# Reordering the opening of a four-layer graph network by hand: chunk 0's transfer first, degrees ahead of the norms, W1's tile on bytes of its own, masks later

## Chip, cores, metric

One core of a Trainium2 chip. The metric is the device time of one execution in microseconds (us). Every profile named here covers one execution, with times counted from the start of its span. PE is the matmul engine (PEld its weight loads), DVE the vector, ACT the scalar, POOL the GpSimd and SP the sync engine, which here only issues transfers.

## The reference, cut to what matters

Four layers, each `x = x + layer(relu(layernorm(x)))`, on x of 128 x 64 x 256 (fp32), with one 64 x 64 adjacency. Only layer 0's beginning and layer 1's beginning matter here:

```python
h = jnp.maximum(_layernorm(x, axis=-1), 0.0)
# layer 0
A_norm = A + jnp.eye(n)
deg = jnp.sum(A_norm, axis=0) + jnp.sum(A_norm, axis=1) - jnp.diagonal(A_norm)
dinv = jax.lax.rsqrt(deg)
A_hat = A_norm * dinv[:, None] * dinv[None, :]
agg = jnp.einsum('nm,bmd->bnd', A_hat, features)
h = jax.nn.relu(_batchnorm(agg @ W1.T + b1, g1, be1))   # 256 -> 512, then W2 back to 256
# layer 1: two graph convolutions with adj, then four LSTMs over windows of 1 to 4 steps
# layers 2 and 3: attention with masks made from the causal triangle and from adj
```

The 8,192 rows are worked in 16 chunks of 512 (512 KB each). Before the first product with W1 can start, chunks 0 and 1 must be normalised and aggregated with A_hat.

## The kernel before

A tile framework places the semaphores and orders instructions by its own estimate of time; inside a `manual_schedule` block the named engines keep the program's order among the block's instructions. Before, that held for PE alone.

```python
    for e in range(2):                                   # adjacency: block diagonal, and a second copy
        r = slice(e * T, (e + 1) * T)
        nc.sync.dma_start(adj_bd[r, r], adj)
        nc.scalar.dma_start(adjt_bd[r, r], adj_t)
        nc.sync.dma_start(adj2[r, :], adj)
    with tc.tile_pool(name="setup", bufs=1) as setup:    # freed before W1's tile is made
        ...                                              # an, ant, dg, deg: eight DVE operations
        rsqrt(dinv, deg[:, 3:4], 0.0)                    # two operations on POOL
        nc.vector.tensor_scalar(rows, an, dinv, None, op0=OP.mult)
        nc.tensor.transpose(pt[:, :P], rows, ident)
        nc.vector.tensor_scalar(ahat_t, pt[:, :P], dinv, None, op0=OP.mult)
        ...                                              # mask2, mask3
    # ... bn1, bn2 loads
    def aggregate(src, mat, name):
        for k in range(KD):
            for j in range(NJ):
                for i in range(2):
                    for e in range(2):
                        nc.tensor.matmul(banks[e][half(i), k, j, :], src[half(e), j, f],
                                         mat[half(e), half(e)], start=True, stop=True)
    # ...
        w1_sb = w0.tile([P, KD, H0], F32, name="w1_sb")  # takes over the setup's bytes
        nc.gpsimd.dma_start(w1_sb, w1t.rearrange("(k p) f -> p k f", p=P))
        nc.gpsimd.dma_start(w2_sb, w2t.rearrange("(k p) f -> p k f", p=P))
        with tc.manual_schedule(engines={mybir.EngineType.PE}):
            norm0(0)                                     # load x, stats on DVE, power on POOL, h on ACT
            norm0(1)
            aggregate0(0)
            for c in range(NCH):
                if c + 1 < NCH:
                    aggregate0(c + 1)
                if c + 2 < NCH:
                    norm0(c + 2)
                product1(c)
    # ... layer 1: its small weights on SP, seven LSTM weights of 1 MB each from POOL, x again on SP
```

Of the kernel before, what the change touches and what calls it, by code (L numbers as in the profile page):

```python
# [8 lines left out]
F32 = mybir.dt.float32  # L9
AF = mybir.ActivationFunctionType  # L10
OP = mybir.AluOpType
AX = mybir.AxisListType

P = 128
EPS = 1e-5
NEG = -1e30
# [3 lines left out]
def kernel(  # L20
# [22 lines left out]
    nc = tc.nc  # L43
    B, T, D = x.shape
    H0 = w1t.shape[1]
    KD = D // P
    KH = H0 // P
# [6 lines left out]
    NJ = CH // P  # L54
# [9 lines left out]
    const = ctx.enter_context(tc.tile_pool(name="const", bufs=1))  # L64
# [4 lines left out]
    def bank(name):  # L69
        return psum.tile([P, CH], F32, tag="ps", name=name)  # L70
# [7 lines left out]
    def rsqrt(dst, src, eps):  # L78

        nc.gpsimd.tensor_scalar(dst, src, eps, None, op0=OP.add)  # L80
        nc.gpsimd.tensor_tensor(dst, dst, mhalf[:, : dst.shape[1]], OP.pow)



    adj_bd = const.tile([P, P], F32, name="adj_bd")
    adjt_bd = const.tile([P, P], F32, name="adjt_bd")
    adj2 = const.tile([P, T], F32, name="adj2")
    nc.vector.memset(adj_bd, 0.0)
    nc.vector.memset(adjt_bd, 0.0)
    for e in range(2):  # L90
        r = slice(e * T, (e + 1) * T)
        nc.sync.dma_start(adj_bd[r, r], adj)
        nc.scalar.dma_start(adjt_bd[r, r], adj_t)
        nc.sync.dma_start(adj2[r, :], adj)


    ahat_t = const.tile([P, P], F32, name="ahat_t")

    mask2 = const.tile([P, T], F32, name="mask2")
    mask3 = const.tile([P, 2 * T], F32, name="mask3")  # L100
    with tc.tile_pool(name="setup", bufs=1) as setup:
        an = setup.tile([P, P], F32, name="an")
        ant = setup.tile([P, P], F32, name="ant")
        nc.vector.tensor_add(an, adj_bd, ident)
        nc.vector.tensor_add(ant, adjt_bd, ident)
        deg = setup.tile([P, 4], F32, name="deg")
        dg = setup.tile([P, P], F32, name="dg")
        nc.vector.tensor_mul(dg, an, ident)
        nc.vector.tensor_reduce(deg[:, 0:1], ant, AX.X, OP.add)
        nc.vector.tensor_reduce(deg[:, 1:2], an, AX.X, OP.add)  # L110
        nc.vector.tensor_reduce(deg[:, 2:3], dg, AX.X, OP.add)
        nc.vector.tensor_add(deg[:, 3:4], deg[:, 0:1], deg[:, 1:2])
        nc.vector.tensor_sub(deg[:, 3:4], deg[:, 3:4], deg[:, 2:3])
        dinv = setup.tile([P, 1], F32, name="dinv")
        rsqrt(dinv, deg[:, 3:4], 0.0)
        rows = setup.tile([P, P], F32, name="rows")
        nc.vector.tensor_scalar(rows, an, dinv, None, op0=OP.mult)
        pt = bank("pt_ahat")
        nc.tensor.transpose(pt[:, :P], rows, ident)
        nc.vector.tensor_scalar(ahat_t, pt[:, :P], dinv, None, op0=OP.mult)  # L120

        causal = setup.tile([P, P], F32, name="causal")
        nc.gpsimd.affine_select(
            out=causal, in_=adj_bd, pattern=[[-1, P]], compare_op=OP.is_ge, fill=NEG, base=0,
            channel_multiplier=1,
        )
        for e in range(2):
            r = slice(e * T, (e + 1) * T)
            nc.vector.tensor_copy(mask2[r, :], causal[r, r])
        for i in range(2):  # L130
            nc.vector.tensor_scalar(mask3[:, i * T : (i + 1) * T], adj2, 0.0, NEG, op0=OP.is_equal,
                                    op1=OP.mult)

    bn1_sb = const.tile([P, 3, KH], F32, name="bn1_sb")
    bn2_sb = const.tile([P, 3, KD], F32, name="bn2_sb")
    nc.gpsimd.dma_start(bn1_sb, bn1)
    nc.gpsimd.dma_start(bn2_sb, bn2)


    def layernorm_relu(dst, src, name):  # L140
        st = small.tile([P, NJ, 6], F32, tag="ln_st", name=f"st_{name}")
        mv = small.tile([P, NJ, 2], F32, tag="ln_mv", name=f"mv_{name}")
        for j in range(NJ):
            nc.vector.bn_stats(st[:, j, :], src[:, j, :])
            nc.vector.bn_aggr(mv[:, j, :], st[:, j, :])
        rstd = small.tile([P, NJ], F32, tag="ln_rstd", name=f"rstd_{name}")
        rsqrt(rstd, mv[:, :, 1], EPS)
        nmr = small.tile([P, NJ], F32, tag="ln_nmr", name=f"nmr_{name}")
        nc.vector.scalar_tensor_tensor(nmr, mv[:, :, 0], -1.0, rstd, op0=OP.mult, op1=OP.mult)
        for j in range(NJ):  # L150
            nc.scalar.activation(dst[:, j, :], src[:, j, :], AF.Relu, bias=nmr[:, j : j + 1],
                                 scale=rstd[:, j : j + 1])

    def half(r):
        return slice(r * T, (r + 1) * T)

    def aggregate(src, mat, name):



        banks = [bank(f"agg{e}_{name}").rearrange("p (k j t) -> p k j t", j=NJ, t=T) for e in range(2)]
        for k in range(KD):
            for j in range(NJ):
                for i in range(2):
                    for e in range(2):
                        f = slice(k * P + i * T, k * P + (i + 1) * T)
                        nc.tensor.matmul(banks[e][half(i), k, j, :], src[half(e), j, f],  # L167
                                         mat[half(e), half(e)], start=True, stop=True)
        return [ps.rearrange("p k j t -> p (k j) t") for ps in banks]
# [45 lines left out]
    z2 = {}  # L215
    with tc.tile_pool(name="w0", bufs=1) as w0, tc.tile_pool(name="z1b", bufs=1) as z1b, tc.tile_pool(
        name="l0", bufs=2
    ) as l0:
        w1_sb = w0.tile([P, KD, H0], F32, name="w1_sb")
        w2_sb = w0.tile([P, KH, D], F32, name="w2_sb")  # L220
        nc.gpsimd.dma_start(w1_sb, w1t.rearrange("(k p) f -> p k f", p=P))
        nc.gpsimd.dma_start(w2_sb, w2t.rearrange("(k p) f -> p k f", p=P))
        st1 = w0.tile([P, KH, NCH, 6], F32, name="st1")



        z1, hs, aggs = {}, {}, {}

        def norm0(c):
            xt = l0.tile([P, NJ, D], F32, tag="xt", name=f"xt_{c}", bufs=3)  # L230
            nc.sync.dma_start(xt, xr[c])
            hs[c] = l0.tile([P, NJ, D], F32, tag="h", name=f"h_{c}")
            layernorm_relu(hs[c], xt, f"a{c}")

        def aggregate0(c):
            aggs[c] = l0.tile([P, KD, CH], F32, tag="agg", name=f"agg_{c}")
            dst = aggs[c].rearrange("p k (j e t) -> p e (k j) t", e=2, t=T)
            for e, ps in enumerate(aggregate(hs.pop(c), ahat_t, f"a{c}")):
                if e == 0:
                    nc.vector.tensor_copy(dst[:, e], ps)  # L240
                else:
                    nc.scalar.copy(dst[:, e], ps)

        def product1(c):
            agg = aggs.pop(c)
            lo = res.tile([P, KD, CH], F32, tag=f"r{c}", name=f"z1a_{c}")
            hi = z1b.tile([P, KH - KD, CH], F32, tag=f"z{c}", name=f"z1b_{c}")
            z1[c] = [lo[:, m, :] for m in range(KD)] + [hi[:, m, :] for m in range(KH - KD)]
            for m in range(KH):
                ps = bank(f"z1_{c}_{m}")  # L250
                for k in range(KD):
                    nc.tensor.matmul(ps, w1_sb[:, k, m * P : (m + 1) * P], agg[:, k, :],  # L252
                                     start=(k == 0), stop=(k == KD - 1))
                nc.scalar.activation(z1[c][m], ps, AF.Identity, bias=bn1_sb[:, 0, m : m + 1])
                nc.vector.bn_stats(st1[:, m, c, :], z1[c][m])
            z2[c] = lo

        def product2(chunks, by_block):
# [12 lines left out]
            for c in chunks:  # L271
                for m in range(KD):
                    nc.vector.tensor_scalar(z2[c][:, m, :], banks[c, m], bn2_sb[:, 0, m : m + 1], None,
                                            op0=OP.add)
                    nc.vector.bn_stats(st2[:, m, c, :], z2[c][:, m, :])

        with tc.manual_schedule(engines={mybir.EngineType.PE}):
            norm0(0)
            norm0(1)
            aggregate0(0)  # L280
            for c in range(NCH):
                if c + 1 < NCH:
                    aggregate0(c + 1)
# [3 lines that stand above are left out]
            sc1, sh1 = bn_params(st1, bn1_sb, w0, "bn1")  # L287
            product2([0, 1], True)
            for c in range(2, NCH):
                product2([c], False)  # L290
# [4 lines left out]
    with tc.tile_pool(name="w1", bufs=1) as w1, tc.tile_pool(name="l1", bufs=2) as l1:  # L295
# [42 lines left out]
        def convolutions(c, hT):  # L338
# [10 lines left out]
            yield  # L349
            h = l1.tile([P, NJ, D], F32, tag="g", name=f"h1_{c}", bufs=3)  # L350
            layernorm_relu(h, xs[c], f"b{c}")

            agg = l1.tile([P, KD, CH], F32, tag="g", name=f"agg1_{c}", bufs=3)
            for e, ps in enumerate(aggregate(h, adjt_bd, f"b{c}")):
                nc.vector.tensor_copy(
                    agg.rearrange("p k (j e t) -> p e (k j) t", e=2, t=T)[:, e], ps)
# [390 lines left out]
```

## Time and profile before

| | us |
|---|---|
| time, median of 4 runs beside the changed kernel's | 2162.64 (2160.51 to 2163.86) |
| first profiled run (a quick one: the span) | 2149.8 |
| second profiled run (label before_again: the span) | 2161.5 |
| first product starts, in the two profiles | 20.73, 20.58 |
| first product ends (next PE work starts) | 27.77, 29.57 |
| layer 0's last matmul ends | 259.52, 260.56 |
| layer 1's first aggregation starts | 284.81, 294.22 |

Lines of the chain of waits read: start us, us, what. The names are tiles: xt is a chunk of x, st its statistics and mv their aggregate (mean and variance), rstd and nmr the scale and shift made from them, h the normalised chunk, agg the aggregate with A_hat (ahat_t), z the product with W1, adj_bd and adjt_bd the adjacency and its transpose. DMA issue lines read: tile, issuing queue, count, KB each, median us from issue to landing. How the small transfers fared in the first 10 us of the kernel before:

```profile
xt<-in_x_dram SPq DMA_DIRECT2D x3, 512.0 KB, 5.0
adj_bd<-in_adj_dram SPq DMA_DIRECT2D x2, 16.0 KB, 2.3
```

### The profile page before, as it was taken

To read this page: it belongs to the slowest core of one execution; us is meant where nothing else is said; L and a number is where in the kernel's file an instruction comes from. 1 tells how busy PE (TensorE), PEld (TensorE's weight loads), DVE (VectorE), ACT (ScalarE), POOL (GpSimd) and SP (SyncE) were. 2 spreads that over 40 slices of the span, in tenths; PEclk is the share of its full clock that TensorE was granted. 3 is DMA by queue.
4 is the path that set the end of the run, shared out by engine and by line. 5 is a ranking of instruction groups with operands and counts; after the bars stand their busy time and mean duration, and the time that the engine had idled before them with its cause. 6 is when DMAs were issued, how large, how long until landed. Compare 5 with 4: busy or idle time off the path is not lost.

```text
span 2149.8 us, 29237 instructions
## 1 busy us (share of the span) xinstructions
PE 2064.2 (96%) x12421; PEld 1293.3 (60%) x12421; DVE 842.9 (39%) x1843; ACT 796.8 (37%) x1449; POOL 171.3 (8%) x224
## 2 busy tenths in 40 slices
PE   6999879999999999999999999999999799999996
PEld 3444344684675576567468467557647666666664
DVE  5644433323323323323332332332222266666664
ACT  5654223333334324333333333433333344444442
POOL 3100100000001001000000000100000012221110
PEclk9999989999999999999999999999999999999998
DMA  3100130000000000000000000000000100000000
GB/s 120 60 1 1 45 147 11 10 1 11 11 1 11 11 1 10 5 7 0 11 10 1 10 11 1 0 1 1 0 0 1 35 11 21 21 21 21 21 21 30
DMA packets 30145, 38.17 MB, mean 18 GB/s; under 512 B 1856, under 2 KB 27456, under 8 KB 30016
## 3 DMA queue, kind: packets, MB, share of 16 engines
q1 hardware_dynamic: 27600, 27.89, 4.0%
q0 software_dynamic: 2256, 8.40, 1.0%
q8 instruction: 97, 1.59, 0.3%
q14 instruction: 32, 0.26, 0.0%
q10 hardware_dynamic: 160, 0.03, 0.0%
HBM read 27.93 MB, written 8.39 MB: 17 GB/s over the span
## 4 chain that ended last, share of the span: by engine, by line
PE 80%; issue 10%; DVE 6%; POOL 2%; DMA 1%; SPq 0%; ACT 0%; POOLq 0%; DVEq 0%; ACTq 0%
PE g L404 33%; PE g L411 17%; PE z L252 5%; PE z L269 5%; PE p_q L535 3%; PE u L374 3%; PE v L362 3%; PE p_k L535 3%; PE tr L558 1%; PE agg_b L167 1%; DMA xt<-in_x_dram 1%; DVE s L549 1%; PE o L675 1%; PE o L620 1%; DVE s L652 1%
## 5 line engine op out<-in xcount | busy, mean ns | idle before, releaser
L404 PE MATMUL g<-hT,wih 128*128 128x256 f32 (+2 forms) x2496 | 829.8, 484 | 3.9 <-DVE hT L435 2.7
L404 PEld LDWEIGHTS g<-hT,wih 128*128 128x128 f32 x2496 | 464.8, 188 | 315.7 <-issue 182.1
L417 ACT ACTIVATE gate<-g,bias 128x256 f32<-128x256 f32 (+2 forms) x624 | 350.3, 562 | 808.1 <-PE g L411 640.9
L411 PE MATMUL g<-hs,whh 128*128 128x256 f32 (+2 forms) x1536 | 435.8, 437 | 0.0
L411 PEld LDWEIGHTS g<-hs,whh 128*128 128x128 f32 x1536 | 291.3, 190 | 132.2 <-issue 62.0
L421 DVE TENSOR_TENSOR cell<-cell,gate 128x256 f32<-128x256 f32 (+2 forms) x96 | 48.7, 508 | 442.5 <-ACT gate L417 442.5
L426 DVE TENSOR_TENSOR cell<-gate,gate 128x512 f32<-128x512 f32 (+2 forms) x80 | 48.2, 603 | 205.3 <-ACT gate L417 205.3
L252 PE MATMUL z<-agg,w_sb 128*128 128x512 f32 x256 | 113.8, 598 | 1.9 <-DMA w_sb<-in_w1t_dram 1.2
L269 PE MATMUL z<-h,w_sb 128*128 128x512 f32 x256 | 110.0, 592 | 0.0
L427 ACT ACTIVATE gate<-cell 128x256 f32<-128x256 f32 (+2 forms) x176 | 89.9, 511 | 51.0 <-DVE cell L426 40.3
L445 POOL COPY hn<-hT 128x512 f32<-128x512 f32 x32 | 35.8, 1196 | 777.8 <-DVE hT L435 777.8
L435 DVE TENSOR_TENSOR hT<-gate,gate 128x512 f32<-128x512 f32 (+2 forms) x80 | 48.0, 600 | 113.9 <-PE g L404 96.8
L269 PEld LDWEIGHTS z<-h,w_sb 128*128 128x128 f32 x256 | 48.6, 190 | 61.2 <-issue 57.6
L252 PEld LDWEIGHTS z<-agg,w_sb 128*128 128x128 f32 x256 | 47.4, 190 | 57.1 <-issue 53.8
L430 DVE TENSOR_TENSOR hs<-gate,gate 128x256 f32<-128x256 f32 (+2 forms) x96 | 47.7, 497 | 69.9 <-ACT gate L427 49.6
L420 DVE TENSOR_TENSOR gate<-gate,gate 128x256 f32<-128x256 f32 (+2 forms) x96 | 47.8, 498 | 55.7 <-ACT gate L417 55.7
L543 POOL TENSOR_TENSOR s<-s,mx 128x256 f32<-128x256 f32 (+1 forms) x32 | 40.3, 1259 | 339.0 <-DVE mx L542 252.1
L530 ACT COPY v<-v 128x512 f32<-128x512 f32 x64 | 37.0, 578 | 76.6 <-PE v L527 76.6
L535 PE MATMUL p_q<-hT,w_sb 128*128 128x512 f32 x128 | 61.9, 606 | 0.3 <-DVE hT L180 0.3
L535 PE MATMUL p_k<-hT,w_sb 128*128 128x512 f32 x128 | 60.1, 592 | 0.0
L527 PE MATMUL v<-w_sb,hT 128*128 128x256 f32 x256 | 59.5, 386 | 0.0
L535 PE MATMUL p_q<-hT,wqk_sb 128*128 128x512 f32 x128 | 57.9, 595 | 0.4 <-DVE hT L180 0.4
(153 smaller groups left out, 1960.3 us busy)
## 6 DMA issues: line engine op xcount, KB each, us to landing
xt<-in_x_dram SPq DMA_DIRECT2D x32, 512.0 KB, 4.0
out_dram<-o SPq DMA_DIRECT2D x16, 512.0 KB, 2.9
wih<-in_wih_t_dram POOLq DMA_DIRECT2D x4, 1024.0 KB, 12.4
whh<-in_whh_t_dram POOLq DMA_DIRECT2D x3, 1024.0 KB, 17.1
w_sb<-in_w_dram SPq DMA_DIRECT2D x1, 768.0 KB, 4.4
wqkv_sb<-in_wqkv_dram SPq DMA_DIRECT2D x1, 768.0 KB, 4.1
w_sb<-in_w1t_dram POOLq DMA_DIRECT2D x1, 512.0 KB, 4.5
w_sb<-in_w2t_dram POOLq DMA_DIRECT2D x1, 512.0 KB, 7.6
```

Source lines behind the costliest of these rows:

```text
L252: nc.tensor.matmul(ps, w1_sb[:, k, m * P : (m + 1) * P], agg[:, k, :], start=(k == 0), stop=(k == KD - 1))
L269: nc.tensor.matmul(banks[c, m], w2_sb[:, k, m * P : (m + 1) * P], h1[c][:, k, :], start=(k == 0), stop=(k == KH - 1))
L362: nc.tensor.matmul(ps, wg0_sb[:, k, m * P : (m + 1) * P], agg[:, k, :], start=(k == 0), stop=(k == KD - 1))
L374: nc.tensor.matmul(ps[:, i, :], v[:, k, j * P : (j + 1) * P], wg1_sb[:, k, :], start=(k == 0), stop=(k == KD - 1))
L404: nc.tensor.matmul(banks[q][:, :n].rearrange("p (j w e) -> p j w e", w=nw, e=2), wi[:, k, o], hv[:, k, :, cols, :], start=(k == 0), stop=( ...
L411: nc.tensor.matmul(banks[q][:, :n], wh[:, k, o], hs[:, k, :n], start=False, stop=(k == KD - 1))
L417: nc.scalar.activation(g[q], banks[q][:, :n], AF.Tanh if q == 2 else AF.Sigmoid, bias=bs[:, q * KD + c : q * KD + c + 1])
L421: nc.vector.tensor_mul(cell[c], cell[c], g[1])
L426: nc.vector.tensor_mul(cell[c], g[0], g[2])
L427: nc.scalar.activation(g[2], cell[c], AF.Tanh)
L527: nc.tensor.matmul(ps[:, i, :], hT[:, k, j * P : (j + 1) * P], w[:, k, first : first + D], start=(k == 0), stop=(k == KD - 1))
L535: nc.tensor.matmul(ps, w[:, k, m * P : (m + 1) * P], hT[:, k, :], start=(k == 0), stop=(k == KD - 1))
```

## The change

The intent: start everything that the first product waits for earlier. Chunk 0's transfer goes first on SP; A_hat's degrees go ahead of the norms on DVE; the setup's tiles get bytes of their own so that W1 can be loaded at the start; the masks of layers 2 and 3 are named later; the second adjacency copy goes; and the aggregation loops over j outside k, so that PE can follow ACT's h piece by piece.

```diff
-        for k in range(KD):
-            for j in range(NJ):
+        for j in range(NJ):
+            for k in range(KD):
...
-        nc.sync.dma_start(adj2[r, :], adj)
...
-    ) as l0:
+    ) as l0, tc.tile_pool(name="setup", bufs=1) as setup:
...
+        with tc.manual_schedule(engines={mybir.EngineType.PE, mybir.EngineType.DVE,
+                                         mybir.EngineType.Pool, mybir.EngineType.SP}):
+            xt = load0(0)
+            for e in range(2):
+                r = slice(e * T, (e + 1) * T)
+                nc.sync.dma_start(adj_bd[r, r], adj)
+                nc.scalar.dma_start(adjt_bd[r, r], adj_t)
+            nc.gpsimd.dma_start(w1_sb, w1t.rearrange("(k p) f -> p k f", p=P))
+            an, dinv = degrees(setup)
+            mv, rstd = ln_stats(xt, "a0")
+            normalized(setup, an, dinv)
+            ln_apply(hs[0], xt, mv, rstd, "a0")
+            norm0(1)
+            nc.gpsimd.dma_start(bn1_sb, bn1)
+            nc.gpsimd.dma_start(bn2_sb, bn2)
+            nc.gpsimd.dma_start(w2_sb, w2t.rearrange("(k p) f -> p k f", p=P))
         with tc.manual_schedule(engines={mybir.EngineType.PE}):
-            norm0(0)
-            norm0(1)
             aggregate0(0)
+            masks(setup)
```

(Cut: the split of the norm into `ln_stats` and `ln_apply`, of the setup into `degrees`, `normalized` and `masks`, and mask3 made from the block-diagonal copy.)

More of the change, by code (lines that the diff above doesn't have):

```diff
@@ L86 @@
     adjt_bd = const.tile([P, P], F32, name="adjt_bd")
-    adj2 = const.tile([P, T], F32, name="adj2")
     nc.vector.memset(adj_bd, 0.0)
     nc.vector.memset(adjt_bd, 0.0)
-    for e in range(2):
-        r = slice(e * T, (e + 1) * T)
-        nc.sync.dma_start(adj_bd[r, r], adj)
-        nc.scalar.dma_start(adjt_bd[r, r], adj_t)
-        nc.sync.dma_start(adj2[r, :], adj)
     ahat_t = const.tile([P, P], F32, name="ahat_t")
@@ L100, with degrees @@
     mask3 = const.tile([P, 2 * T], F32, name="mask3")
-    with tc.tile_pool(name="setup", bufs=1) as setup:
+    bn1_sb = const.tile([P, 3, KH], F32, name="bn1_sb")
+    bn2_sb = const.tile([P, 3, KD], F32, name="bn2_sb")
+    def degrees(setup):
         an = setup.tile([P, P], F32, name="an")
@@ L115, with normalized @@
         rsqrt(dinv, deg[:, 3:4], 0.0)
+        return an, dinv
+    def normalized(setup, an, dinv):
         rows = setup.tile([P, P], F32, name="rows")
@@ L120, with masks @@
         nc.vector.tensor_scalar(ahat_t, pt[:, :P], dinv, None, op0=OP.mult)
+    def masks(setup):
         causal = setup.tile([P, P], F32, name="causal")
@@ L129, with ln_stats @@
             nc.vector.tensor_copy(mask2[r, :], causal[r, r])
-        for i in range(2):
-            nc.vector.tensor_scalar(mask3[:, i * T : (i + 1) * T], adj2, 0.0, NEG, op0=OP.is_equal,
-                                    op1=OP.mult)
-    bn1_sb = const.tile([P, 3, KH], F32, name="bn1_sb")
-    bn2_sb = const.tile([P, 3, KD], F32, name="bn2_sb")
-    nc.gpsimd.dma_start(bn1_sb, bn1)
-    nc.gpsimd.dma_start(bn2_sb, bn2)
-    def layernorm_relu(dst, src, name):
+            for i in range(2):
+                nc.vector.tensor_scalar(mask3[r, i * T : (i + 1) * T], adj_bd[r, r], 0.0, NEG,
+                                        op0=OP.is_equal, op1=OP.mult)
+    def ln_stats(src, name):
         st = small.tile([P, NJ, 6], F32, tag="ln_st", name=f"st_{name}")
@@ L147, in layernorm_relu, with ln_apply @@
         rsqrt(rstd, mv[:, :, 1], EPS)
+        return mv, rstd
+    def ln_apply(dst, src, mv, rstd, name):
         nmr = small.tile([P, NJ], F32, tag="ln_nmr", name=f"nmr_{name}")
@@ L152, in layernorm_relu @@
                                  scale=rstd[:, j : j + 1])
+    def layernorm_relu(dst, src, name):
+        ln_apply(dst, src, *ln_stats(src, name), name)
     def half(r):
@@ L217, with load0 @@
         name="l0", bufs=2
-    ) as l0:
+    ) as l0, tc.tile_pool(name="setup", bufs=1) as setup:
         w1_sb = w0.tile([P, KD, H0], F32, name="w1_sb")
         w2_sb = w0.tile([P, KH, D], F32, name="w2_sb")
-        nc.gpsimd.dma_start(w1_sb, w1t.rearrange("(k p) f -> p k f", p=P))
-        nc.gpsimd.dma_start(w2_sb, w2t.rearrange("(k p) f -> p k f", p=P))
         st1 = w0.tile([P, KH, NCH, 6], F32, name="st1")
         z1, hs, aggs = {}, {}, {}
-        def norm0(c):
+        def load0(c):
             xt = l0.tile([P, NJ, D], F32, tag="xt", name=f"xt_{c}", bufs=3)
@@ L232, in norm0 @@
             hs[c] = l0.tile([P, NJ, D], F32, tag="h", name=f"h_{c}")
+            return xt
+        def norm0(c):
+            xt = load0(c)
             layernorm_relu(hs[c], xt, f"a{c}")
```

## The prediction

> **What bounds the kernel now.** I read the page's busy row first, then the chain of waits over the first 60 us, the waits of that stretch, the timeline of single instructions, and the windows around the start of layer 1. The page says that TensorE is the bound almost everywhere:
>
> ```profile
> PE 2064.2 (96%) x12421; PEld 1293.3 (60%) x12421; DVE 842.9 (39%) x1843; ACT 796.8 (37%) x1449; POOL 171.3 (8%) x224
> ```
>
> So work saved on DVE, ACT or the DMA queues pays only where PE stands still. The change touches the opening, and the chain there (start us, duration, what) reads:
>
> ```profile
> 3.39 4.19 DMA xt<-in_x_dram
> ...
> 13.15 0.28 DVE rows L117
> ...
> 13.93 1.05 POOL rstd_a L81
> ...
> 15.50 0.26 DVE ahat_t L120
> ...
> 16.05 4.55 DMA w_sb<-in_w1t_dram
> 20.60 0.14 issue
> 20.73 7.11 PE z L252 x16
> 27.84 1.09 PE agg_a L167 x64
> 28.93 7.06 PE z L252 x16
> ```
>
> The reader is to see that from 20.73 us on the chain is PE alone, 8.15 us a chunk (7.06 + 1.09), and that everything before it is latency: x lands at 7.6 us because its transfer was issued at 3.39 us behind the adjacency's four; A_hat is ready only at 15.76 us; W1's transfer starts only then. The waits (waiter, awaited, us in total, times, longest) show why W1 is last:
>
> ```profile
> POOL w_sb L221 <- DVE ahat_t L120: 1.1, 1, 1.1
> PE z L252 <- DMA w_sb<-in_w1t_dram: 1.2, 1, 1.2
> ```
>
> W1's tile takes over the bytes of the setup's tiles, so its transfer is held until A_hat is done. But PE misses only 1.2 us by it: the aggregations of chunks 0 and 1, both ahead of the first product in PE's order, end at 19.57 us:
>
> ```profile
> 15.90 3.67 PE L167 MATMUL agg_a<-ahat_t,h 64*64 64x64 f32 x128 [1.94 <-ACT h L151]
> 17.97 0.59 ACT L242 COPY agg<-agg_a 128x512 f32<-128x512 f32 x1 [0.70 <-PE agg_a L167]
> ```
>
> So taking W1 off the setup's bytes is alone worth at most 1.2 us; the rest must come from earlier norms and an earlier A_hat. The whole prize is bounded: of 2163 us, the product cannot start more than some 10 us earlier, 0.5%.
>
> The other place is the start of layer 1, as the loop order of the aggregation changes for all layers. There ACT's four activations per chunk pace PE:
>
> ```profile
> 284.16 4.04 ACT L151 ACTIVATE h<-xs,nmr_b,rstd_b 128x256 f32<-128x256 f32 x8 [14.40 <-DVE nmr_b L149]
> ...
> 288.25 1.03 PEld L167 LDWEIGHTS agg_b<-adjt_bd,h 64*64 64x64 f32 x40 [0.17 <-ACT h L151]
> ```
>
> After ACT's last h, PE still has 40 of an aggregation's 64 instructions to do, because k is the outer loop and the whole second half of the features comes after the last j.
>
> **What the Trainium skill says.** (1) "DMA: Bandwidth & Descriptors", section "Issuing engines are not separate DMA queues": transfers of all issuing engines run on the same 16 DMA engines and interleave. The trace agrees: three x chunks queued back to back at 3.39 us moved at 341 to 368 GB/s and the DMA row was full. So adjacency rows issued behind chunk 0 do not overtake it, and W1, issued early, competes with x. (2) The same page, "Anatomy of one DMA", gives a fixed 2.0 us plus bytes over 436 GB/s, which is 3.2 us for 512 KB; the trace has 3.6 at the least, 4.0 in the median and 4.19 for chunk 0. I use the trace's. (3) "TensorE: Matmul & The Clock Gate", Part 1: the array starts at half clock and is released after some 3.4 us of activity. The 128 opening instructions took 3.67 us, 1.8 per aggregation, against 1.09 later, which agrees in kind, though the clock column reads 1.00 there; at the start of layer 1 the column itself shows it, 0.50 in 284 to 288 us and 1.00 from 289.5 us. (4) The same page, "Architectural detail", has DVE and ACT as strict first-in-first-out queues. The trace agrees: A_hat's last operation, ready once the transpose ended at 13.96 us, waited on DVE behind chunk 1's stats and the scale of chunk 1 (which waited on POOL) until 15.42 us. A fixed DVE order is thus a real lever, and a risk.
>
> **The change part by part.** I follow the new program order, with durations from the old timeline.
>
> Chunk 0 first: SP's first issue slot is 0.73 us, so x of chunk 0 lands at 0.73 + 4.19 = 4.9 us instead of 7.6. The adjacency's two diagonal blocks are issued at about 1.4 and 2.0 us. Alone they took 2.3 us (page, DMA issues); now they stand behind 512 KB in the same queue, so I put their landing, D, at 5.2 us.
>
> DVE degrees: in the old timeline from 10.39 to 12.12 us with 0.33 us of masks between, so 1.4 us: done at 6.6. POOL's dinv (0.24 + 0.59 and gaps) takes 1.0 us: 7.6. Meanwhile DVE does the stats of chunk 0, four at 0.31 and four at 0.08 and the tail, 1.7 us: 8.3. Dinv is hidden behind these. Rows 0.28, transpose 0.53 with its hand-over, A_hat 0.34: ready at 9.5. POOL's rstd (0.24 + 1.05 and gaps, 1.4): 9.7; nmr 0.16 with hand-over: 9.95. ACT's four h take 2.07 us: first at 10.6, last at 12.05. So A_hat is just off the path, the norm of chunk 0 sets it. PE starts at 10.6 instead of 15.9, and with j outermost it has only 16 instructions left after the last h (0.46 us at the slow rate): aggregation 0 ends at 12.5.
>
> Chunk 1: its stats stand on DVE behind chunk 0's nmr: 9.95 + 1.7 = 11.65; POOL 1.4: 13.1; nmr: 13.25; ACT's h until 15.35; aggregation 1 ends at 15.35 + 0.46 = 15.8, and the first product starts at **15.9 us**. Its other inputs are earlier: ACT's copy of aggregate 0 ends by 13.1, DVE's by 14.0 even behind nmr 1; W1, issued from POOL at about 1.5 us, needs 4.55 us and at most two more for sharing, so 8 us. That wait of PE vanishes.
>
> Gain of the opening: 20.73 - 15.9 = 4.8 us. Against it stands the clock: PE's activity is now ACT-paced with some 1.3 us of idleness between the aggregations. At layer 1 full clock came about 4 us after the first matmul, here 5.3 us pass, so the product probably starts at full rate; if one 3.4 us window still runs at half clock, 1.7 us are lost. I take 0.7 (0.4 of that).
>
> Loop order at layer 1: 16 instead of 40 instructions after the last h, 24/40 of 1.09 us = 0.6 us gained. In the steady state nothing: PE's waits for h in layer 1 come to 10.3 us, all of it one wait, that opening.
>
> Masks and the dropped adj2: two transfers of 16 KB go, six small DVE operations and one on POOL (1.2 us together as an estimate from 0.1 to 0.2 us each before) move to a stretch where DVE is busy 4.5 of 10 us: nothing on the path. The third x buffer comes free at 12.05 instead of 14.3 us, so chunk 3 comes earlier too: DVE's 4.15 us wait for it at 25.5 us should shrink, also off the path.
>
> Sum: 4.8 - 0.7 + 0.6 = 4.7 us. 2162.75 - 4.7 = 2158.0 us, 0.2% less.
>
> **The rivals.** *The queue delays the adjacency.* DVE in fixed order now waits for the adjacency before it touches chunk 0, and chunk 0, W1 and chunks 1 and 2 (2 MB, about 6 us at 350 GB/s) are all asked for in the first 4 us. If D is 7 us instead of 5.2, everything moves by 1.8: gain 2.9 us, 2159.9. For it: one queue, shared engines. Against it: only 512 KB stand ahead of the adjacency.
> *Only the W1 wait pays.* If chunk 1's norm, now serial behind chunk 0's on DVE and POOL, eats the earlier start, 1.2 us remain: 2161.6. Against it: in the working above the serial order still ends aggregation 1 3.7 us earlier.
> *Cold clock.* The full 1.7 us lost: 2159.0.
> *Given back downstream.* The start of layer 1 waits for x behind the LSTM weights (chain: 14.97 us of transfer from 262.98 us). These are issued when layer 0's last product ends, so they move with it and the gain passes. But the compiler's scheduler still orders ACT, and DVE and POOL after the opening; a different order there could move either way by some 3 us.
> *Better than worked out.* If the adjacency lands with its unloaded 2.3 us at 4.3 us and the clock is up: gain 6.3 us, 2156.5.
>
> **Range and chances.** The rivals span 2156.5 to 2161.6; with the scheduler's freedom and about 1 us between runs (2162.53 to 2163.86 before) I take 2153 to 2162. A gain over 2% would be 43 us, over twice all the time before the first product: 0.01. Slower by 2% has no mechanism: 0.01. Within 2%: 0.98.
>
> **What would show it.** Right: x of chunk 0 landing near 5 us, the first aggregation near 10.6, the first product near 15.9 us, no wait of PE for W1, 7.1 us for the first sixteen instructions of the product, 16 instead of 40 weight loads after the last h at layer 1, and the first product's shift, less any clock loss, found again at layer 0's end. Wrong: `an` waiting for the adjacency beyond 6 us, a first product of over 8 us (clock), DVE's copy of aggregate 0 as the last wait ahead of it, or a layer 1 start that moved otherwise than layer 0's end.

## The result, and the profile after

2163.64 us (median of 4, 2160.52 to 2164.30) against 2162.64: ratio 1.0003, 95% interval 0.9986 to 1.0020. Ratios are the mean time of one kernel's runs over that of the other's of the same rounds, so not quite the ratio of these medians. A second set, six runs of the changed kernel on another chip, gave 0.9998 (0.9982 to 1.0014). The change is worth nothing that the clock on the wall can see, and the time lies 1.6 us above the predicted range; the second set's median, 2161.55 us, lies just inside it. The forecast gain of 4.7 us is in neither set.

The chain of waits over the opening of the changed kernel:

```profile
1.83 5.72 DMA adj_bd<-in_adj_dram
...
7.68 0.19 DVE mask L131
...
7.90 0.29 DVE an L100
...
9.35 0.20 DVE mask L129
...
10.11 0.18 DVE mv_a L140
...
13.35 0.16 DVE nmr_a L147
13.51 0.67 DVE st_a L139 x2
14.18 0.08 DVE mv_a L140
...
17.11 1.01 POOL rstd_a L81
...
18.35 0.61 ACT h L149
...
19.00 2.18 PE agg_a L168 x64
21.18 9.22 PE z L255 x16
30.40 1.09 PE agg_a L168 x64
```

Four things are to be seen. Chunk 0 did land early, at 4.22 us, but the chain does not run through it: it starts with the adjacency, issued at 1.83 us and 5.72 us under way. Masks stand in front of `an` and among the degrees, although the program names them later. The st_a row at 13.51 us begins 3.1 us of stats in which chunk 2's alternate with chunk 1's. And the first product takes 9.22 us where the profile before has 7.11. The two mv_a rows are for later: an aggregate directly behind the stats that it reads takes 0.18 us, one with another chunk's stats in between 0.08.

Issue to landing in the first 10 us of the changed kernel, to be read against the 2.3 us of before:

```profile
xt<-in_x_dram SPq DMA_DIRECT2D x3, 512.0 KB, 6.1
w_sb<-in_w1t_dram POOLq DMA_DIRECT2D x1, 512.0 KB, 6.2
adjt_bd<-in_adj_t_dram ACTq DMA_DIRECT2D x2, 16.0 KB, 4.3
adj_bd<-in_adj_dram SPq DMA_DIRECT2D x2, 16.0 KB, 5.1
```

The same 16 KB now take 4.3 to 5.1 us, on SP's queue and on ACT's.

The 9.22 us is the clock. In the timeline of PE's weight loads the rate changes in the middle of the first product (start us, us, then, in brackets, the idle time ahead):

```profile
24.68 0.34 PEld L255 LDWEIGHTS z<-agg,w_sb 128*128 128x128 f32 x1 [0.52 <-issue]
...
25.95 0.19 PEld L255 LDWEIGHTS z<-agg,w_sb 128*128 128x128 f32 x1 [0.24 <-issue]
```

Both the load and the gap halve between these two. The clock column of the page reads 1.00 all along here, so it is only the durations that show it.

Side by side, from the traces (two profiles of each kernel, unedited; the first product lasts from its start to the next work on PE, and the LSTM stretch from its first instruction on PE to the end of its last):

| us | before | before again | after | after again |
|---|---|---|---|---|
| chunk 0 lands | 7.58 | 7.42 | 4.22 | 4.19 |
| adjacency lands (second block) | 4.17 | 4.24 | 7.55 | 6.49 |
| W1 lands | 20.60 | 20.44 | 7.51 | 7.39 |
| first aggregation starts | 15.90 | 15.73 | 14.20 | 13.16 |
| first product starts | 20.73 | 20.58 | 21.11 | 20.07 |
| first product lasts | 7.04 | 9.00 | 9.22 | 9.22 |
| rest of layer 0 | 231.75 | 230.98 | 230.98 | 230.98 |
| layer 0 ends | 259.52 | 260.56 | 261.31 | 260.28 |
| from there to layer 1's first aggregation | 25.29 | 33.66 | 33.86 | 33.64 |
| first aggregation to first v | 4.53 | 4.72 | 3.83 | 3.88 |
| LSTM stretch | 1384.14 | 1384.12 | 1384.12 | 1384.13 |

### The profile page after: what moved, and what is told of

Read it like the earlier page. It is cut to its first block, busy times and chain, and to the rows that moved or that the text cites. A ratio compares the mean times of both kernels' runs of the same rounds, so it can differ in the third digit from the quotient of the medians. Undisturbed runs are those within 1.5% of the kernel's fastest.

```text
span 2162.5 us, 29233 instructions
## 1 busy us (share of the span) xinstructions
PE 2070.5 (96%) x12421; PEld 1298.1 (60%) x12421; DVE 842.7 (39%) x1845; ACT 797.0 (37%) x1449; POOL 171.0 (8%) x224
## 4 chain that ended last, share of the span: by engine, by line
PE 80%; issue 10%; DVE 6%; POOL 2%; DMA 1%; SPq 0%; ACT 0%; POOLq 0%; DVEq 0%; ACTq 0%
PE g L423 33%; PE g L430 17%; PE z L255 5%; PE z L272 5%; PE p_q L554 3%; PE u L393 3%; PE v L381 3%; PE p_k L554 3%; PE tr L577 1%; DMA xt<-in_x_dram 1%; PE agg_b L168 1%; PE o L694 1%; DVE s L568 1%; PE o L639 1%; DVE s L671 1%
## 5 line engine op out<-in xcount | busy, mean ns | idle before, releaser
L149 ACT ACTIVATE h<-xs,nmr_b,rstd_b 128x256 f32<-128x256 f32 x64 | 34.5, 590 | 69.1 <-DVE nmr_b L147 69.1
```

## The experiments

**The changed kernel again (after_again), unedited.**

> The changed kernel again, unedited. Opening: the adjacency lands at 7.5 us, first product starts at 21.1 us within 0.3 us, if its lateness is the program's own. The first product's sixteen instructions took 9.2 us; if that is the clock[...], they may take anything from 7.1 to 9.3 us here. Start of layer 1, from the end of layer 0 to its first aggregation: 25.3 us in the trace of before, 33.9 us in the trace of after. If the difference is luck of the transfers (theory: variance), this run can show 25 to 30 us; if it is the change's doing (rival), it shows 33 to 35 us again.

2161.55 us, 0.9998 of before (0.9982 to 1.0014). Table above. The opening is the program's own, except that the adjacency lands at 6.49 instead of 7.55 us and everything up to the product moves with it: 13.58 us from its landing to the product's start, 13.56 in the first profile. The clock was cold again. The start of layer 1 took 33.6 us again.

**The kernel before again (before_again), unedited.**

> The kernel before, unedited, for a second profile. Opening as in the first: first product at 20.7 us, its end at 27.8 us. Start of layer 1: in the first profile 25.3 us from the end of layer 0 to the first aggregation, in four profiles of the changed kernel and its variants 33 to 34 us. Theory (the first profile of before caught a rare quick passage; the change does nothing there): 32 to 34 us here too. Rival (the change slows the start of layer 1 by 8 us): 25 us again.

2163.63 us, 1.0008 (0.9993 to 1.0023), which also shows how far a kernel differs from itself. Its start of layer 1 takes 33.66 us (layer 1's first aggregation starts at 294.22 us, against 284.81 in the first profile), so the 25.29 of the first profile was a quick passage and not a merit of the kernel before. The chain lines for x of chunk 1 there, first profile and then the second:

```profile
262.98 14.97 DMA xt<-in_x_dram
```

```profile
265.23 22.14 DMA xt<-in_x_dram
```

The second profile also shows that the kernel before can start its first product cold:

```profile
15.88 4.56 DMA w_sb<-in_w1t_dram
20.44 0.14 issue
20.58 9.07 PE z L252 x16
```

In the first profile the same wait and nearly the same start led to 7.11 us.

**W1's transfer after the degrees (a_w1_later).**

```diff
-            nc.gpsimd.dma_start(w1_sb, w1t.rearrange("(k p) f -> p k f", p=P))
             an, dinv = degrees(setup)
+            nc.gpsimd.dma_start(w1_sb, w1t.rearrange("(k p) f -> p k f", p=P))
```

> W1's transfer issued after A_hat's degrees instead of at the start. Theory (W1's 512 KB compete with the adjacency on the 16 DMA engines): the adjacency's second block lands at 4.5 to 5.2 us instead of 7.55, and the first product starts 2.4 to 3 us earlier, at 18.1 to 18.7 us. Rival (the adjacency stands behind chunk 0 in SP's own queue, W1 does not matter): it lands at 7 us or later and the first product stays at 21 us. W1 then lands at 13 to 15 us, before it is needed in both.

2159.68 us, 0.9990 (0.9972 to 1.0009). The adjacency lands at 5.51 us, a little later than the theory's band, and the product starts at 19.09 us, 13.58 us after it. W1 lands at 12.72 us, in time. So W1's early transfer costs 1 to 2 us of the adjacency's delay, but not all: 5.51 is still 1.3 us above the 4.2 of the kernel before. The rival is out. This is one profile, but six profiles with the changed kernel's order of transfers have the landing at 6.49 to 7.71 us, and 5.51 lies clear of them.

**The adjacency ahead of chunk 0 on SP (a_adj_first).**

```diff
-            xt = load0(0)
             for e in range(2):
                 ...                        # the four adjacency transfers
+            xt = load0(0)
```

> In the changed kernel, the adjacency's two transfers ahead of chunk 0's on SP, nothing else. Theory (the adjacency is late because 512 KB stand ahead of it in its queue): it lands at 4.2 to 4.7 us, chunk 0 at 5.5 to 6.2 us, degrees run from 4.7 us and the first product starts at 17.6 to 18.5 us. Rival (W1's transfer alone delays it): it still lands at 6 us or later and the first product starts at 19.5 us or later.

2160.16 us, 0.9990 (0.9975 to 1.0005). The adjacency lands at 6.08 us, chunk 0 at 7.38 us, the product starts at 19.63 us: the rival's numbers. The two blocks differ within this one run: the first, issued at 1.05 us, took 2.1 us, and the second, under way from 1.68 us, took 4.4; W1 was asked for at 1.29 us, between them. In c_open2 below, with x at the same times but W1 later, the blocks take 1.9 to 2.0 us. Going first in its own queue does not protect a small transfer while W1's 512 KB are asked for from another engine. Against the 6.49 to 7.71 us of the other order, 6.08 is too near to show a gain.

**Chunk 0's stats ahead of the degrees (a_stats_first).**

```diff
-            an, dinv = degrees(setup)
             mv, rstd = ln_stats(xt, "a0")
+            an, dinv = degrees(setup)
```

> In the changed kernel, chunk 0's stats ahead of the degrees on DVE, nothing else. Theory (DVE stands idle from chunk 0's landing at 4.2 us to the adjacency's at 6.5 to 7.5 us, because the fixed order has the degrees first): stats run in that gap, and the first product starts 1.5 to 2.2 us earlier relative to the adjacency's landing (13.6 us after it in three profiles): 11.4 to 12.1 us after it. Rival (POOL or ACT or chunk 1 sets the pace): 13 us or more after it.

2161.06 us, 0.9992 (0.9976 to 1.0009). The product starts 12.65 us after the adjacency's landing: 0.9 us gained, between the two expectations. DVE's idle gap was real, but with it filled the chain goes through A_hat and chunk 1's stats, which are mixed with chunk 2's as before. The missing 0.6 us to the theory lie ahead of that. The scheduler slipped the masks in among chunk 0's stats, and each pair made DVE wait for an adjacency block (the number in brackets):

```profile
5.94 0.29 DVE L131 TENSOR_SCALAR mask<-adj_bd 64x64 f32<-64x64 f32 x2 [0.55 <-DMA adj_bd<-in_adj_dram]
...
7.01 0.29 DVE L131 TENSOR_SCALAR mask<-adj_bd 64x64 f32<-64x64 f32 x2 [0.39 <-DMA adj_bd<-in_adj_dram]
```

So the last stats came after the landing, and `an` started 0.96 us behind it instead of 0.35.

**Masks and chunk 2's norm pinned behind the opening (a_pinned).**

```diff
             norm0(1)
+            masks(setup)
             ...                            # bn1, bn2, W2
+            norm0(2)                       # inside the fixed block, last
         with tc.manual_schedule(engines={mybir.EngineType.PE}):
             aggregate0(0)
-            masks(setup)
```

> The masks and chunk 2's norm put at the end of the fixed block, so that the scheduler cannot slip them in among degrees and chunk 1's stats on DVE. Theory (these foreign operations delay DVE): 0.2 us of masks before the degrees, 0.4 in them and 1.6 us of chunk 2's stats go, and the first product starts 1.6 to 2.3 us earlier, at 18.8 to 19.5 us. Rival (POOL's power and ACT's h set the pace): it starts at 20.5 to 21.1 us. The adjacency still lands near 7.5 us.

2161.68 us, 0.9997 (0.9979 to 1.0015). The second aggregation ends 12.17 us after the adjacency instead of 13.63, 1.5 us earlier, as the theory has it. But the product starts only 0.7 us earlier (12.86 us after the adjacency). The timeline shows what took the place:

```profile
18.94 0.67 DVE L243 COPY agg<-agg_a 128x512 f32<-128x512 f32 x1
...
19.71 2.05 PE L255 MATMUL z<-agg,w_sb 128*128 128x512 f32 x2 [0.70 <-issue]
```

DVE's copy of aggregate 0, ready since 15.2 us, now stands behind the masks and four of chunk 2's stats, and the product starts as it ends. One mis-ordered queue was exchanged for another.

**Idle products to warm the clock (a_warm).**

```diff
             xt = load0(0)
+            for i in range(40):
+                nc.tensor.matmul(bank(f"warm_a{i}")[:, :P], ident, ident, start=True, stop=True)
             ...
             aggregate0(0)
+            for i in range(10):
+                ...                        # the same again
```

> Forty idle products of the identity with itself on PE from 3 us on and ten between the first two aggregations; nothing reads them. Theory (PE's clock is at half rate when the first product starts): the first product's sixteen instructions take 7.1 us instead of 9.2, an aggregation is bound by ACT's h alone, and the first product ends at 27.9 to 28.3 us instead of 30.3. Rival (something else slows them, such as transfers or evacuation): they still take 9 us or more.

2166.27 us, 1.0023 (1.0004 to 1.0042): worse by some 0.2%. The first product took 7.06 us, so the clock theory holds for the 2.2 us. But the forty products were not free:

```profile
2.71 11.62 PE L285 MATMUL warm_a<-ident 128*128 128x128 f32 x80 [2.71 <-POOL ident masks.py:199]
```

They held up A_hat's transpose until 14.16 us, the product started at 22.3 us and ended at 29.39 us (theory: 27.9 to 28.3), and the scheduler's DVE order, shifted by them, made PE wait 3.2 us for a copy of a later aggregate.

**The loop order alone, in the kernel before (b_j_outer).**

> The kernel before with the loop order of the aggregation alone (j outside k). Theory: 16 instead of 40 instructions follow the last h where ACT paces PE; at the start of layer 1 the time from the first aggregation to the first v falls from 4.5 to 3.8-3.9 us, and the opening's two aggregations do not change by more than 0.3 us, because A_hat and not h is last there. Rival (the interleaved bank order costs PE something): an aggregation in the steady state takes more than 1.09 us per 64 instructions.

2161.02 us, 0.9992 (0.9977 to 1.0006). First aggregation to first v at layer 1: 4.05 us against 4.53 and 4.72, so 0.5 to 0.7 us gained, a little less than expected (3.8 to 3.9). The opening moves by under 0.3 us (product at 20.50), the rest of layer 0 is 231.26 us. No cost to PE is seen. Right in kind, and too small for the time to show.

**All delays of the opening together (c_open, c_open_warm, c_open2).** Fixed DVE order through both copies of the first two aggregates, then chunk 2, then masks; four stats and then four aggregates instead of pairs; W1 after the degrees. In c_open chunk 0 heads SP's queue, with chunks 1 and 2 right behind it, and the adjacency is on other queues:

```diff
-                nc.sync.dma_start(adj_bd[r, r], adj)
-                nc.scalar.dma_start(adjt_bd[r, r], adj_t)
+                nc.scalar.dma_start(adj_bd[r, r], adj)
+                nc.gpsimd.dma_start(adjt_bd[r, r], adj_t)
...
+            mv, rstd = ln_rest(*ln_bn(xt, "a0"), "a0")
+            xt1 = load0(1)
+            rows = normalized_rows(setup, an, dinv)
+            st1x = ln_bn(xt1, "a1")         # chunk 1's stats fill the wait for the transpose
+            normalized_cols(rows, dinv)
+            ln_apply(hs[0], xt, mv, rstd, "a0")
+            mv1, rstd1 = ln_rest(*st1x, "a1")
+            ln_apply(hs[1], xt1, mv1, rstd1, "a1")
+            aggregate0(0)
+            aggregate0(1)
+            ...                             # W2
+            norm0(2)
+            masks(setup)
```

(Cut: the issue of W1 and of the small parameters, the loop's bounds, and, in c_open and c_open_warm alone, the identity for transposes made after the transfers are issued.)

> The opening with the found delays taken out together: chunk 0 alone at the head of SP's queue, the adjacency on ACT's and POOL's queues, W1 after the degrees, DVE in one fixed order up to the masks (degrees, four stats and then four aggregates per chunk, both copies of aggregates 0 and 1, then chunk 2, then masks). Theory (the prediction's chain holds once transfers and DVE's order are as it supposed): adjacency at 4.2 to 5 us, first product at 14.2 to 15.5 us, and as the clock is cold, its sixteen instructions take 8.6 to 9.3 us, ending at 23 to 24.8 us; end of layer 0 at 254 to 256 us against 258.8 to 261.3 so far. Rival (a chain of POOL and ACT keeps the first product at 19 us whatever DVE does): first product at 18 us or later.

2160.14 us, 0.9988 (0.9973 to 1.0003). The adjacency lands at 7.65 us, no better than in the changed kernel: other queues do not help it beside three x chunks. Its transposed copy, on POOL's queue, lands later still, and the degrees wait for that:

```profile
2.25 6.44 DMA adjt_bd<-in_adj_t_dram
...
14.23 4.14 PE agg_a L184 x128
18.38 8.12 PE z L271 x16
```

The product starts at 18.31 us, the rival's number, and layer 0 ends at 257.9 us, outside the theory's band. But the rival's cause is not what is seen: from the last block's landing at 8.69 us the product follows after 9.6 us. The prediction's chain has 10.7 us there. This is no clean test of it, since chunk 1's stats now run ahead of chunk 0's scale; what is shown is that the stretch is 4 us shorter than the changed kernel's 13.6.

> The same with sixteen idle products before the degrees' end and four between the first two aggregations. Theory (clock): the first product takes 7.0 to 7.6 us instead of 8.6 to 9.3, and ends at 21.5 to 23.5 us, 1 to 2 us before that of c_open. Rival (the idle products hold up A_hat's transpose or the aggregations by as much as the clock gives): its end is no earlier than that of c_open.

2158.96 us, 0.9986 (0.9971 to 1.0001). The product itself takes 7.1 us instead of 8.12, as the clock theory has it, but starts 1.5 us later (four idle products stand between the aggregations and delay the second). It ends at some 27.0 us, and the next PE work, which waits 0.44 us for h, starts at 27.43 against 26.42. The rival's outcome.

c_open2 asks for the small transfers before any large one, as the kernel before did:

```diff
+            for e in range(2):
+                r = slice(e * T, (e + 1) * T)
+                nc.sync.dma_start(adj_bd[r, r], adj)
+                nc.scalar.dma_start(adjt_bd[r, r], adj_t)
             xt = load0(0)
```

> As c_open, but the adjacency's four small transfers first (SP and ACT), then x of chunk 0 and 1, then W1 after the degrees; no large transfer is asked for before the small ones. In c_open the adjacency, on queues of its own but beside two x chunks, landed at 7.65 us, and the first product started 10.65 us after it. Theory (the adjacency must be asked for before any large transfer): it lands at 4.1 to 4.5 us, chunk 0 at 6 to 6.6 us, and the first product starts at 14.6 to 15.6 us. Rival (x of chunk 0 now comes as late as in the kernel before, 7.4 us, and sets the pace): first product at 16 to 17 us. In both the end of layer 0 is at 254 to 257 us.

2155.01 us, 0.9966 (0.9949 to 0.9982). The adjacency lands at 3.64 us, chunk 0 at 5.96, the product starts at 14.41 us, layer 0 ends at 253.07 us, even somewhat better than the theory. The chain of its opening:

```profile
2.93 5.13 DMA xt<-in_x_dram
...
8.08 1.41 DVE st_a L141 x4
9.49 0.25 DVE ahat_t L122
...
10.50 3.90 PE agg_a L185 x128
...
14.41 7.13 PE z L272 x16
```

The adjacency is off the chain, which now runs through chunk 1's landing at 8.06 us. The two aggregations run without a gap for 3.9 us, and the product behind them is warm without any help. That the closed gap warms it is not shown: c_best below repeats it (4.14 us, then 7.07), but c_open has 4.14 us without a gap and then 8.12.

**The start of layer 1 (a_x_first, b_x_first), and both together (c_best).** That start took 25 to 34 us in the table, a scatter that hides some 3 us elsewhere, and it is itself a cost. x of chunks 0 and 1 goes ahead of the LSTM weights, and these follow on SP:

```diff
+        for c in range(SUP):
+            early[c] = l1.tile([P, NJ, D], F32, tag="xt", name=f"xt1_{c}", bufs=2)
+            nc.sync.dma_start(early[c], xr[c])
...
-            nc.gpsimd.dma_start(w, wih_t[p].rearrange("(k p) f -> p k f", p=P))
+            nc.sync.dma_start(w, wih_t[p].rearrange("(k p) f -> p k f", p=P))
```

> The changed kernel; at the start of layer 1 x of chunks 0 and 1 is queued on SP ahead of the LSTM weights, which follow in the same queue instead of POOL's. Theory (the start of layer 1 is late because x shares the 16 DMA engines with 7 MB of weights): from the end of layer 0 x of chunk 1 lands after 7 to 10 us instead of 26 to 27, the first aggregation starts after 15 to 19 us instead of 33 to 34, and the run is 14 to 18 us shorter: 2144 to 2149 us. Rival (the weights are then too late for the LSTM): PE waits for wih or whh by more than 5 us and under 8 us are gained.

2144.96 us, 0.9922 (0.9906 to 0.9939). x of chunk 1 lands 10.05 us after the end of layer 0, just outside the band, instead of 27.0, the first aggregation starts after 15.78 us. PE's waits around that start (waiter, awaited, us in total, times, longest), in the changed kernel and then here:

```profile
PE agg_b L168 <- ACT h L149: 14.9, 1, 14.9
PE c L331 <- DMA bg_sb<-in_bg_dram: 9.4, 1, 9.4
```

```profile
PE agg_b L168 <- ACT h L149: 6.2, 2, 5.6
PE c L331 <- DMA bg_sb<-in_bg_dram: 4.7, 1, 4.7
```

No wait for wih or whh appears in its place. The theory holds, with one limit: the order and the weights' queue were changed together, and the wait for bg_sb, which is ahead of x in its queue, also fell. So it is shown that the weights in flight delay the others, but not which of the two changes is needed.

> The kernel before with x ahead of the LSTM weights, nothing else. Theory (the scatter of the kernel before, 2151.8 to 2166 us, and the 8 us between its two profiles are that start of layer 1): 2144 to 2149 us with a spread under 3 us, the first aggregation of layer 1 15 to 17 us after the end of layer 0. And if the change itself is worth nothing, the same time within 2 us as a_x_first (0.9922 of before).

2148.25 us (2145.87 to 2149.16), 0.9931 (0.9916 to 0.9945). The first aggregation follows layer 0 after 16.10 us, as expected. The spread is 3.3 us against 3.9 for before in this set, only slightly narrower and not under 3, so the start of layer 1 is not shown to be the whole of the scatter. Against a_x_first's 0.9922 the difference is 0.0009, about 2 us, with intervals that overlap: no gain of the change is shown. Layer 0 ends at 260.38 us here and at 260.44 in a_x_first.

> c_open2 with x ahead of the LSTM weights at the start of layer 1. If both gains add: a_x_first's 0.9922 of before less the 3 to 5 us by which c_open2's layer 0 ends earlier than the changed kernel's: 2139 to 2143 us, 0.989 to 0.991 of before. Rival (the earlier opening is given back at the start of layer 1): 0.992, no better than a_x_first.

2138.65 us (2138.11 to 2140.47), 0.9889 (0.9875 to 0.9904): the quickest kernel, 24 us under before. The two gains add; layer 0 ends at 253.24 us and layer 1's first aggregation follows after 16.08 us.

## Why the prediction was wrong, step by step

The prediction was 4.7 us of gain, and nothing was gained. Its frame held: PE is the bound, the opening is latency, the prize is a few tenths of a per cent, the W1 wait of PE vanished, the rest of layer 0 passed a shift on unchanged (230.98 us in three profiles of four). For "run on the same 16 DMA engines and interleave" its trace gave only transfers of one queue; a_adj_first is the run that shows it across queues. Its sum failed by these terms. In the first profile the product starts 5.2 us after the predicted 15.9: 2.4 by term 1 and 2.9 by term 2. Then it runs cold, which is term 3.

1. **"I put their landing, D, at 5.2 us."** Measured 7.55 and 6.49: 1.3 to 2.4 us. The first rival named this and gave it too little weight ("only 512 KB stand ahead of the adjacency"), and the prediction's own "W1, issued early, competes with x" was not carried over to the adjacency. What counts is not what stands ahead in the queue but every large transfer in flight: without W1 5.51, ahead of chunk 0 but beside W1 6.08, on other queues but beside three x chunks 7.65, and ahead of all large ones 3.64 us.
2. **"1.4 us: done at 6.6", then 1.7 us of stats, then chunk 1's 1.7 us.** From landing to product 10.7 us were predicted and 13.56 and 13.58 measured. By the chain of after: the degrees end 2.2 us after the landing (0.8 more, of which 0.7 are masks in front of them and among them), chunk 0's stats take 2.2 us (each aggregate directly behind the stats that it reads, 0.5 more), and chunk 1's take 3.1 us (mixed with chunk 2's, 1.4 more). Sum 2.7 of the 2.9; a_pinned, which takes the masks and chunk 2 out, ends the second aggregation 1.5 us earlier. The failed assumption was that a fixed block keeps others out. It only orders its own instructions; the scheduler slipped masks and chunk 2 in between, and so "masks later" was not even carried out. c_open, with these removed and chunk 1's stats moved up, takes 9.6 us from the last block's landing.
3. **"I take 0.7 (0.4 of that)"** for the clock. The product lost 2.2 us against a warm one in both profiles. That is more than the worst case given, 1.7. The reason given, that more time passes from the first matmul than at layer 1, was wrong: full rate came 11 us after the first aggregation's start, where 5.3 us were to do. PE was idle for 2.6 us between the two aggregations, but this is not shown to be the cause: in c_open PE ran without a gap from 14.23 us and was at half rate until about 20.5. In sixteen profiles the first product took 7.0 to 7.1 us in six, two of them with idle products ahead, and 8.1 to 9.2 in ten. Part of this is no loss of the change, since before_again lost 2.0 us too; the profile from which I predicted was a lucky one in this, as in its start of layer 1.
4. **The 0.6 us at layer 1** held: first aggregation to first v 3.83 and 3.88 us against 4.53 and 4.72; alone it gave 0.5 to 0.7.

So the expected gain went into contention (1), into operations that the scheduler moved in and dependent pairs of stats and aggregate (2), and into the clock (3). With 1 and 2 mended and a product that was warm, c_open2 gains the predicted amount and more: its product starts at 14.41 us and its time is 0.9966 of before. It does so by another route than the change, with the adjacency ahead of chunk 0 and W1 after the degrees.

What stays open: why the adjacency took 7.55 us in one profile and 6.49 in the next of the same program; what makes the rare quick start of layer 1; and what decides whether the first product starts warm.

## What to carry to other kernels

Ask for the small transfer that a chain begins with before any large one, on whatever queue; a transfer "issued at once" because nothing holds it back any more can delay the one that matters. A block of fixed order is only fixed against itself: read the instruction order that results, and look for what was moved in. And take no prediction from one profile where a microsecond counts; two profiles of the same kernel differed by 12 us here (spans of 2149.8 and 2161.5 us), most of it at one start that nobody had touched.

## What the Trainium skill lacked or had wrong

- "DMA: Bandwidth & Descriptors", "Issuing engines are not separate DMA queues": right that transfers of all issuing engines share the 16 DMA engines (in a_adj_first W1, from POOL, held up a block on SP: 4.4 us instead of 2.1), but the section has no figure for the latency of a small transfer beside large ones. The runs: 16 KB take 2.3 us with hardly a large one under way (median), 5.1 us behind and beside 512 KB transfers, 4.7 us on ACT's queue and 6.2 us on POOL's with three x chunks on SP's.
- The same page, "Anatomy of one DMA": fixed 2.0 us plus bytes over 436 GB/s, a fit for transfers issued from gpsimd, gives an estimate of 3.2 us for 512 KB. W1, issued from POOL, took 4.1 us in a_w1_later and 3.9 in c_open, where hardly anything else was under way. The section has no fit for transfers issued by SP: chunk 0 at the head of SP's queue took 3.5 us (0.73 to 4.22), and the median of the opening's x transfers was 5.0 to 6.1 us when several were in flight.
- "TensorE: Matmul & The Clock Gate", Part 1: some 3.4 us of sustained activity release the clock. c_open2 agrees (3.9 us of aggregations without a gap, then a product of 7.06 us at full rate from its start). c_open does not: without a gap PE was at half rate for some 6.3 us, from 14.23 to about 20.5. Nor is there a figure for a cold array with short gaps: two aggregations of 2.2 us with 2.6 us between them left PE at half rate until about 25.5 us, 11 us after the first of them began. The trace's clock column read 1.00 throughout that, so durations must be read too.
- No page has a figure for the cost on DVE of an aggregate placed right behind the stats that it reads: 0.18 us for the aggregate instead of 0.08. Four such pairs took 2.2 us in the changed kernel, four stats and then four aggregates 1.6 us from the first stats to the next operation in c_open (10.06 to 11.65).
